# Keys and queries of finished batches made inside the state space chunks, convolution diagonals streamed, pieces laid out anew: one core of Trainium2

## The chip, the cores and the metric

The kernel runs on one core of a Trainium2 chip, in float32 throughout. The metric is the device time of one execution in microseconds (us). The engines are PE (TensorE: matmuls; its weight loads are listed as PEld), DVE (VectorE), ACT (ScalarE), POOL (GpSimd) and SP (SyncE, which issues all DMAs here). Each runs its own list of instructions in order, and they wait for one another by semaphores.

## The reference, cut to what matters

x has 4 batches of 384 channels and 64 x 64 positions (4096 tokens).

```python
def _gn(v, G=32): ...                    # normalize in 32 groups of channels, per batch
# layer 0: state space layer over the 4096 tokens of a batch
xn = layernorm(_gn(x)); xb, z = split(xn @ in_proj_w.T)      # 2 x 768 channels
xc = silu(causal_conv4(xb) + conv_b)                         # 4 taps, per channel
dt, B, C = split(xc @ x_proj_w.T); dt = softplus(dt @ dt_w.T + dt_b)
h = exp(dt * A) * h + (dt * xc) * B                          # 16 states a channel, token by token
x = x + out_proj((sum_n h * C + xc * D) * silu(z))
# layer 1: attention over a 7 x 7 window around each position, 12 heads of 32
q, k, v = split(w_qkv @ _gn(x) + b_qkv); q = q * 32**-0.5    # k, v padded by 3, edges repeated
x = x + w_proj @ softmax(q . k_window + rel_bias) . v_window + b_proj
```

## The kernel before

**State space layer** (`state_space_layer`, line 328). A batch is cut into 11 chunks of 372 or 376 tokens, so there are 44 chunks. A chunk has 24 groups: 6 blocks of 128 channels (d) times 4 groups of 4 states (g). For a group, `drive` (776) multiplies dt * xc with B, on DVE or POOL as the table DRIVES says (quarters are states of a group); `decay` (794) makes exp(dt * A) on ACT, one of three PSUM banks at a time; `scan` (805) runs four recurrences on DVE; `times_c` (820) multiplies with C on POOL; `sums` (834) adds up the states by transposing matmuls on PE. Around it, per chunk: normalization (`gn`, `ln_*`), `in_proj` (569) with weights streamed from DRAM by `load_w` (565), `conv` (602) as four matmuls with diagonal matrices `dcv` that stay in SBUF, `x_proj`, `dt_mm`, `softplus`, `gate`, `out_proj` (689), `residual` (706), which stores the layer's result x1 to DRAM.

The order of the work is written out by hand: every piece has a tick in the table AT (line 40), relative to its chunk's first scan; 16 ticks are one group, 384 one chunk. `put` (447) collects the pieces, they are sorted by tick, and each engine gets its instructions in that order. `Written` (133; line 143 is where every instruction is recorded, hence the L143 in the profile) keeps this order on each engine, SP's DMAs among them. PSUM has three banks `mm` for all matmuls but the scans' (`bank`, 430).

Statistics of the next batch's x (`x_stats`, `x_norm`) and of a finished batch's x1 (`out_norm`) are made within the chunks, in eight steps over PE, DVE, POOL and ACT (`stats_phases`, 247). Values of the attention for batches that are finished are made within the chunks too: three tiles of 128 tokens a chunk, from chunk 13 on (`value_load` 485 to `value_store` 513, the loop over `tiles`), and go to DRAM (`vdr`).

**Attention** (`attention_layer`, 999). There are 32 stripes of 8 rows (512 tokens), each of 12 units: 4 pairs of 8 x 8 blocks times 3 sets of 4 heads. A unit's steps are spread over the loop at 1261: `scores` (1183: lg matmuls on PE, bias and minimum on DVE, exp on ACT), `divide` (1207: POOL) one step later, `turn` (1212: transposes pt on PE, copies pT on DVE and ACT) two steps later, `weigh` (1223: ov on PE) three later. Beside the units, `pieces` (1149) sets matmuls for other stripes: values (where they are not made yet), three `key` (1074) and two `query` (1104) pieces of stripe s+2, the third query of s+1, and three `project` pieces of s-1. A piece is three matmuls of 128 x 512 in the single bank `mm`; one float32 matmul is two records in the profile. `key` is followed by copies on POOL that repeat edges and hand rows to the neighbouring stripes. `load_x` brings x1 of stripe s+3, and POOL normalizes it (`gn`, 1055). `load_v` (1246) brings the values of a pair of blocks in four DMAs.

Of the kernel before, what the change touches and what calls it, by code (L numbers as in the profile page):

```python
# [8 lines left out]
F32 = mybir.dt.float32  # L9
# [5 lines left out]
P = 128  # L15
# [21 lines left out]
HBUFS = 6  # L37


AT = dict(  # L40
    load_x=(-766,),
    gn=(-732, -677, -738),
    ln_mean=(-636,),
    ln_centre=(-633,),
    ln_square=(-611, -560, -597),
    ln_var=(-545, -545, -544),
    ln_rstd=(-520,),
    ln_scale=(-516,),
    halo=(-551,),
    load_w=(-473, -410, -373, -353, -313, -350, -153, -130, -112, -106, -67, -22),  # L50
    in_proj=(-416, -404, -346, -331, -272, -290, -122, -108, -84, -43, -41, -1),
    in_bias=(-402, -388, -344, -328, -268, -283, -122, -104, -65, -40, -36, 49),
    conv=(-374, -299, -281, -232, -218, -226),
    conv_bias=(-358, -296, -280, -230, -162, -217),
    silu_x=(-245, -127),
    x_proj=(-123, -114),
    x_rows=(-112,),
    dt_mm=(-93, -59),
    softplus=(-87, -58),
    load_b=(-77, -46, -18, -33),  # L60
    load_c=(-6, 17, 47, 65),
    silu_z=(4, 79),
    gate=(142, 234, 270, 319, 399, 457),
    out_proj=(500, 518, 565, 589, 571, 605),
    load_res=(430, 476, 582),
    residual=(529, 591, 621),
    out_stats=(678, 680, 704),
    dt_to_bank=(-50, 10, 100, 156, 201, 264),
    dt_times_x=(-43, 31, 110, 163, 208, 297),
    dtx_copy=(-16, 49, 126, 165, 231, 317),  # L70
    skipped=(17, 109, 145, 173, 251, 301),
    turned_out=(111, 179, 233, 293, 363, 410),
    back=(125, 224, 247, 306, 386, 447),
    carry=(
        -4, -32, -1, 12, 34, 59, 38, 72, 102, 116, 126, 142, 171, 188, 188, 221, 239, 238,
        250, 276, 290, 296, 318, 326,
    ),
    last_states=(
        25, 39, 49, 73, 82, 97, 112, 134, 155, 159, 173, 202, 209, 238, 239, 257, 280, 292,
        310, 324, 344, 357, 372, 388,  # L80
    ),
    times_c=(
        31, 40, 65, 89, 107, 114, 131, 135, 182, 191, 197, 205, 226, 242, 251, 265, 298, 302,
        320, 345, 354, 373, 396, 398,
    ),
    sums=(
        47, 70, 91, 97, 120, 134, 143, 175, 183, 217, 222, 227, 247, 262, 282, 283, 312, 318,
        342, 347, 378, 390, 400, 406,
    ),
    x_stats=(-37, 71, 89, 302),  # L90
    x_norm=(24, 252, 265, 310, 322, 334, 336, 342, 352),
    out_norm=(332, 414, 421, 427, 436, 466, 473, 479, 499),
    value_load=(31, 188, 279),
    value_norm=(68, 213, 341),
    value_mm=(84, 236, 362),
    value_out=(125, 243, 385),
    value_store=(217, 245, 400),
# [3 lines left out]
    (-5, 1, "G", 0, 4), (-4, 0, "V", 0, 3), (-4, 0, "V", 3, 1), (7, 2, "V", 0, 4),  # L101
    (14, 3, "G", 0, 4), (52, 4, "G", 3, 1), (54, 4, "V", 0, 2), (63, 4, "V", 2, 1),
    (71, 6, "V", 0, 4), (76, 5, "V", 3, 1), (78, 5, "G", 0, 3), (89, 7, "G", 0, 4),
    (112, 8, "V", 0, 4), (132, 10, "G", 0, 2), (134, 9, "G", 2, 2), (136, 9, "V", 0, 2),
    (136, 10, "V", 2, 1), (147, 11, "G", 0, 4), (152, 10, "G", 3, 1), (173, 12, "V", 0, 4),
    (191, 14, "V", 0, 4), (200, 13, "G", 0, 4), (222, 15, "G", 0, 4), (252, 16, "V", 0, 4),
    (256, 17, "V", 0, 1), (257, 18, "V", 0, 3), (264, 17, "G", 1, 3), (276, 18, "G", 3, 1),
    (292, 19, "G", 0, 4), (298, 20, "V", 0, 4), (323, 22, "V", 0, 3), (325, 22, "V", 3, 1),
    (330, 21, "V", 2, 2), (332, 21, "G", 0, 2), (350, 23, "G", 0, 4),
# [50 lines left out]
def two_layers(  # L160
# [147 lines left out]
    have_values = set()  # L308
# [19 lines left out]
    def state_space_layer(eng):  # L328
# [5 lines left out]
        with ExitStack() as es:  # L334
# [6 lines left out]
            w_dt = wt.tile([P, DI], F32, name="w_dt")  # L341
            dcv = wt.tile([P, ND, KC, P], F32, name="dcv")
# [3 lines left out]
            w_v = wt.tile([P, NJ, C], F32, name="w_v")  # L346
            fill = wt.tile([QB, KN], F32, name="fill")
            ge.memset(fill, MASKED)
            with tc.tile_pool(name="fold", bufs=1, side="right") as fold, tc.tile_pool(
# [16 lines left out]
                for k in range(3):  # L366
                    dq.dma_start(w_dt[32 * k : 32 * k + DTR, :], dt_wT)
# [33 lines left out]
                for m in range(2 * ND):  # L401
                    dq.dma_start(wdr[m], w_in[:, :, m * P : (m + 1) * P])
                for d in range(ND):
                    for k in range(KC):
                        ve.tensor_scalar(
                            dcv[:, d, k, :], ident, w_cv[:, d, k : k + 1], None, ALU.mult
                        )

# [107 lines left out]

            def xn_of(X, j):
                return made[X]["xn"][:, j, HALO : HALO + chunks[X][3]]
# [82 lines left out]

            def conv(X, d):
                T = chunks[X][3]
                made[X]["cv", d] = ps = bank()
                xb = made[X].pop(("xb", d))
                for k in range(KC):
                    te.matmul(
                        ps[:, :T], dcv[:, d, k, :], xb[:, k : k + T],
                        start=(k == 0), stop=(k == KC - 1),
                    )  # L610
                done(xb)

# [45 lines left out]
            def dt_mm(X, half):  # L658
                T = chunks[X][3]
                for k in range(3):  # L660
# [4 lines left out]
                        ps[:, :T], w_dt[rows, d * P : (d + 1) * P], made[X]["xd"][rows, :T],  # L665
# [212 lines left out]
            for X in range(len(chunks)):  # L878
# [18 lines left out]
                for d in range(ND):  # L897
                    piece("conv", d, conv, d)
                    piece("conv_bias", d, conv_bias, d)
# [85 lines left out]

            put(-120, dq.dma_start, w_out, out_wT.rearrange("(k p) m -> p k m", p=P))
            put(-120, dq.dma_start, w_v, qkv_wT[:, 2 * C :].rearrange("(k p) m -> p k m", p=P))
            put(
# [10 lines left out]
    def attention_layer(eng, gm1, qkb, pjb):  # L999
# [3 lines left out]
        with ExitStack() as es:  # L1003
# [5 lines left out]
            dq.dma_start(w_qkv, qkv_wT.rearrange("(k p) m -> p k m", p=P))  # L1009
# [64 lines left out]
            def key(s, m, ps):  # L1074
                b, r = of(s)
# [11 lines left out]
                )  # L1087
                own = kt[:, m, PAD : PAD + RB, :]
# [59 lines left out]

            def pieces(s, k):

                b, r = of(s + 2)
                if (b, NPAIR * r) in have_values:
                    table = {
                        0: [(query, s + 1, 2)], 2: [(key, s + 2, 0)], 4: [(key, s + 2, 1)],
                        5: [(project, s - 1, 0)], 6: [(key, s + 2, 2)],
                        7: [(project, s - 1, 1)], 9: [(project, s - 1, 2)],
                        10: [(query, s + 2, 0)], 11: [(query, s + 2, 1)],
                    }
                else:
                    table = {  # L1160
                        0: [(query, s + 1, 2), (value, s + 2, 0)],
                        1: [(value, s + 2, 1)], 2: [(value, s + 2, 2)], 3: [(value, s + 2, 3)],
                        4: [(key, s + 2, 0)], 5: [(project, s - 1, 0)],
                        6: [(key, s + 2, 1)], 7: [(project, s - 1, 1)],
# [191 lines left out]
```

## Time and profile before

| what | us |
|---|---|
| runs of the kernel | 6871.43, 6875.25, 6876.22 (median 6875.25) |
| the profiled execution's own time | 6870.13 |
| its span, first to last instruction | 6868.4 |
| first scan of the state space layer begins | 124.2 |
| its last scan ends | 5145.3 |
| first scores of the attention begin | 5211.7 |

Busy time over the span: PE 6287.1 us (92%), PEld 4236.8 (62%), DVE 5869.3 (85%), ACT 5609.8 (82%), POOL 5710.1 (83%). By stages (us, and the mean granted clock of TensorE as a share of full speed):

| stretch | length | PE | PEld | DVE | ACT | POOL | clock | DMA share |
|---|---|---|---|---|---|---|---|---|
| 124.2 to 5145.3 | 5021.1 | 4518.0 | 3224.5 | 4923.3 | 4548.5 | 4955.5 | 0.96 | 0.32 |
| 5145.3 to 5211.7 | 66.4 | 53.9 | 30.3 | 8.9 | 5.2 | 20.4 | 0.89 | 0.39 |
| 5211.7 to 6868.4 | 1656.7 | 1629.7 | 926.2 | 906.0 | 1016.7 | 726.7 | 1.00 | 0.31 |

The busy time of an engine is the time in which at least one of its instructions runs. Instructions of one engine overlap by about 0.1 us, and matmuls are pipelined and their ends modelled, so a sum of durations is more than the time they take together. Registers, branches, semaphores and DMA issues are not counted as busy. `h<-h,BC` reads: tile h is written from tiles h and BC. The chain that ended last goes through DVE's scans (h, 24% of the span), PE's matmuls into mm (24%) and POOL's h (9%); since it follows each wait to the one who ended it, it wanders between engines that are all nearly full.

### The profile page before, as it was taken

Reading aid. Unit: us, or ns where it says so; the run is one execution under the profiler, and the core shown is the slowest. Engines: PE = TensorE matmul, PEld = TensorE weight load, DVE = VectorE, ACT = ScalarE, POOL = GpSimd, SP = SyncE. Lnnn points to the kernel's source line nnn. Section 1 sums busy time; section 2 is a strip of 40 time slices with the busy share of each in tenths; the row PEclk is TensorE's granted clock in tenths of the full one; section 3 lists DMA queues with packets and bytes.
Section 4 is the critical chain, followed back from the end, with each engine's and each line's share of the span. In section 5 each row is a group of like instructions: output and inputs, shape, how many; then the busy total and the mean of one; then the engine's idle time right before and its main releaser. Section 6 shows DMA issues by size and latency. Waiting matters only on the chain.

```text
span 6868.4 us, 132032 instructions
## 1 busy us (share of the span) xinstructions
PE 6287.1 (92%) x46986; PEld 4236.8 (62%) x46986; DVE 5869.3 (85%) x10215; ACT 5609.8 (82%) x13919; POOL 5710.1 (83%) x2701
## 2 busy tenths in 40 slices
PE   7898988898999999899999999999969999999999
PEld 4666666666666666666666666666655555555555
DVE  4999999999999999999999999999994555555555
ACT  4898988889999989899999999999974666665556
POOL 2999999999999999999999999999993444444443
PEclk9999999999999999999999999999989999999999
DMA  5233232223333323333333333333313232333332
GB/s 156 83 104 98 96 102 85 96 92 109 104 112 103 107 97 111 103 107 110 109 104 101 102 95 106 97 107 104 95 60 107 95 100 94 97 99 102 105 101 91
DMA packets 502833, 694.86 MB, mean 101 GB/s; under 512 B 51269, under 2 KB 457173, under 8 KB 502045
## 3 DMA queue, kind: packets, MB, share of 16 engines
q1 hardware_dynamic: 502172, 686.41, 31.6%
q8 instruction: 372, 6.09, 0.4%
q14 instruction: 289, 2.36, 0.1%
HBM read 600.76 MB, written 85.65 MB: 100 GB/s over the span
## 4 chain that ended last, share of the span: by engine, by line
PE 39%; DVE 27%; ACT 17%; POOL 9%; issue 6%; DMA 1%; SPq 0%; POOLq 0%; DVEq 0%; ACTq 0%
DVE h L143 24%; PE mm L143 24%; POOL h L143 9%; PE yps L143 5%; ACT da L143 5%; PE pt L143 5%; ACT L143 4%; PE lg L143 3%; PE ov L143 2%; ACT sg L143 1%; ACT dt L143 1%; ACT sz L143 1%; ACT xc L143 1%; DVE dtxps L143 1%; DVE yg L143 1%
## 5 line engine op out<-in xcount | busy, mean ns | idle before, releaser
L143 DVE TENSOR_TENSOR_SCAN h<-da,h 128x373 f32<-128x373 f32 (+1 forms) x4224 | 3650.2, 913 | 90.1 <-ACT da L143 68.9
L143 POOL TENSOR_TENSOR h<-h,BC 128x1488 f32<-128x1488 f32 (+1 forms) x1056 | 3252.1, 3105 | 40.9 <-ACT state L143 24.9
L143 ACT ACTIVATE da<-dt,nega 128x372 f32<-128x372 f32 (+1 forms) x4224 | 2369.2, 570 | 260.4 <-DVE h L143 229.0
L143 POOL TENSOR_TENSOR h<-dtx,BC 128x1488 f32<-128x1488 f32 (+3 forms) x704 | 1770.5, 2526 | 40.5 <-ACT dtx L143 38.7
L143 PE MATMUL yps<-ident,h 128*124 128x128 f32 (+1 forms) x12672 | 1600.3, 279 | 215.9 <-POOL h L143 214.9
L143 PEld LDWEIGHTS yps<-ident,h 128*124 128x124 f32 (+1 forms) x12672 | 1468.1, 143 | 422.2 <-POOL h L143 278.7
L143 PE MATMUL mm<-xn,w_in 128*128 128x372 f32 (+3 forms) x3168 | 1201.1, 519 | 186.2 <-ACT dt L143 165.3
L143 POOL TENSOR_TENSOR sg<-sg,rs 128x784 f32<-128x784 f32 x384 | 573.3, 1493 | 682.4 <-DVE rs L143 554.9
L143 ACT ACTIVATE sg<-sg,mx 128x196 f32<-128x196 f32 x1536 | 685.2, 447 | 463.5 <-DVE mx L143 458.9
L143 PEld LDWEIGHTS mm<-xn,w_in 128*128 128x128 f32 x3168 | 615.0, 205 | 581.2 <-ACT dt L143 215.9
L143 DVE TENSOR_TENSOR h<-dtxps,BC 128x1488 f32<-128x1488 f32 (+6 forms) x836 | 937.6, 1134 | 11.0 <-ACT dtx L143 5.0
L143 DVE CUSTOM_DVE_ANT_0 sg<-lg,bias 128x196 f32<-128x196 f32 x1536 | 464.3, 358 | 277.2 <-PE lg L143 276.9
L143 PE MATMUL mm<-xb,dcv 128*128 128x372 f32 (+1 forms) x2112 | 690.5, 476 | 0.0
L143 ACT ACT_TABLE_LOAD x529 | 678.7, 1283 | 9.6 <-PEq L1341 0.8
L143 PE MATMUL mm<-yg,w_out 128*128 128x372 f32 (+1 forms) x1584 | 531.8, 477 | 0.0
L143 PEld LDWEIGHTS mm<-xb,dcv 128*128 128x128 f32 x2112 | 389.0, 190 | 227.2 <-DVE yg L143 3.3
L143 PE MATMUL mm<-xp,w_qkv 128*128 128x512 f32 x1098 | 501.7, 593 | 0.0
L143 PE MATMUL pt<-ident,sg 128*98 128x128 f32 x3072 | 429.6, 279 | 16.7 <-ACT pT L143 11.3
L143 PEld LDWEIGHTS pt<-ident,sg 128*98 128x98 f32 x3072 | 315.3, 128 | 150.8 <-issue 102.9
L143 PEld LDWEIGHTS mm<-yg,w_out 128*128 128x128 f32 x1584 | 291.3, 191 | 162.4 <-issue 0.6
L143 PEld LDWEIGHTS ov<-pT,vw 98*32 98x32 f32 x12288 | 189.2, 110 | 237.3 <-issue 162.5
L143 POOL COPY kt<-kt 128x210 f32<-128x210 f32 (+1 forms) x384 | 97.3, 286 | 250.7 <-ACT kt L143 244.8
(134 smaller groups left out, 6896.3 us busy)
## 6 DMA issues: line engine op xcount, KB each, us to landing
BC<-bcrows SPq DMA_DIRECT2D x320, 744.0 KB
w_in<-wdr SPq DMA_DIRECT2D x528, 192.0 KB
vw<-vdr SPq DMA_DIRECT2D x512, 147.0 KB
xs<-in_x_dram SPq DMA_DIRECT2D x210, 186.0 KB
xp<-x SPq DMA_DIRECT2D x32, 768.0 KB
o<-x SPq DMA_DIRECT2D x96, 256.0 KB
out_dram<-o SPq DMA_DIRECT2D x96, 256.0 KB
BC<-bcrows SPq DMA_DIRECT2D x32, 752.0 KB
```

What stands on the lines that cost most here:

```text
L143: ins = made(*args, **kw)
```

## The change

There are five parts. One: for batches 0 to 2, as far as chunks are there, a tile of 256 tokens of keys and one of queries is made in each chunk from two chunks after the batch's end on: x1 is loaded, normalized on ACT, multiplied with weights that are loaded 128 columns at a time, evacuated on ACT and stored to DRAM (`kdr`, `qdr`; queries in the order in which blocks read them, with bias and scale). Two: in the attention, a stripe whose keys and queries are there loads them (`load_keys`) at unit 0 two stripes ahead, and has no x1 load, no normalization and no key and query pieces; POOL's edge copies become `surround`. Three: the diagonals `dcv` are stored to DRAM once and loaded per chunk and block (`load_cv`, three buffers); the weights of dt are kept in a third of the room. Four: the loads of `w_qkv` and `w_pj` and the output bias come later. Five: all ticks in AT, and DRIVES, are new.

```diff
 AT = dict(
-    load_w=(-473, -410, -373, -353, -313, -350, -153, -130, -112, -106, -67, -22),
-    in_proj=(-416, -404, -346, -331, -272, -290, -122, -108, -84, -43, -41, -1),
+    load_w=(-556, -419, -340, -366, -306, -365, -138, -149, -106, -103, -67, -32),
+    in_proj=(-411, -388, -340, -343, -251, -321, -128, -134, -80, -33, -46, 23),
...
-    x_norm=(24, 252, 265, 310, 322, 334, 336, 342, 352),
-    out_norm=(332, 414, 421, 427, 436, 466, 473, 479, 499),
+    x_norm=(12, 182, 194, 198, 211, 231, 247, 257, 271),
+    out_norm=(319, 401, 414, 424, 442, 465, 482, 493, 507),
...
+    load_cv=(-473, -346, -314, -235, -259, -344),
+    key_load=(44, 213),
+    key_norm=(93, 69, 126, 276, 234, 288),
+    key_mm=(135, 139, 181, 303, 305, 348),
+    key_out=(143, 150, 191, 307, 315, 358),
+    key_store=(289, 467),
 DRIVES = (
...
+                dcv = fold.tile([P, ND, KC, P], F32, name="dcv")
                 for d in range(ND):
                     for k in range(KC):
                         ve.tensor_scalar(
                             dcv[:, d, k, :], ident, w_cv[:, d, k : k + 1], None, ALU.mult
                         )
+                    dq.dma_start(ddr[d], dcv[:, d, :, :])
...
+            def key_load(cell):
+                b, k = cell["at"]
+                xk = cell["x"] = tile_of([P, NJ, KT], "xk", 1)
+                dq.dma_start(
+                    xk, x1s[b][:, k * KT : (k + 1) * KT].rearrange("(k p) t -> p k t", p=P)
+                )
+            def key_norm(cell, j):
+                g = gm1[cell["at"][0]]
+                v = cell["x"][:, j, :]
+                se.activation(v, v, AF.Identity, scale=g[:, j, 1:2], bias=g[:, j, 2:3])
+            def key_weights(cell, m):
+                w = cell["w", m] = tile_of([P, NJ, P], "wk", 2)
+                at = cell["part"] * C + m * P
+                dq.dma_start(w, qkv_wT[:, at : at + P].rearrange("(k p) m -> p k m", p=P))
+            def key_mm(cell, m):
+                if m != 1:
+                    cell["ps", m // 2] = bank()
+                lo, w = KT if m == 1 else 0, cell.pop(("w", m))
+                for j in range(NJ):
+                    te.matmul(
+                        cell["ps", m // 2][:, lo : lo + KT], w[:, j, :],
+                        cell["x"][:, j, :], start=(j == 0), stop=(j == NJ - 1),
+                    )
...
+            def key_out(cell, m):
...
+                if cell["part"]:
+                    se.activation(
+                        cell["y"][:, m, :], ps[:, lo : lo + KT], AF.Identity,
+                        bias=qkb[:, NJ + m : NJ + m + 1],
+                    )
+                else:
+                    se.activation(
+                        cell["y"][:, m, :].rearrange("p (b r c) -> p r b c", b=NBLK, c=CB),
+                        ps[:, lo : lo + KT].rearrange("p (r b c) -> p r b c", b=NBLK, c=CB),
+                        AF.Identity, bias=qs[:, m : m + 1], scale=HD**-0.5,
+                    )
...
+            def load_cv(X, d):
+                made[X]["cw", d] = w = tile_of([P, KC, P], "cw", CWBUFS)
+                dq.dma_start(w, ddr[d])
...
+            for i, (part, have) in enumerate(((1, have_keys), (0, have_queries))):
+                tiles = [(b, k) for b in range(NB - 1) for k in range(L // KT)]
+                for X in range(len(chunks)):
+                    if not tiles or X < NCHUNK * (tiles[0][0] + 1) + 2:
+                        continue
+                    b, k = tiles[0]
+                    if k % 2 == 0 and X == len(chunks) - 1:
+                        break
+                    cell = {"at": tiles.pop(0), "part": part}
+                    have.add((b, k))
...
+            def load_keys(s):
+                b, r = of(s)
+                dq.dma_start(
+                    q_of(s),
+                    qdr[b][:, r * TX : (r + 1) * TX].rearrange("(k p) t -> p k t", p=P),
+                )
+                for m in range(NJ):
+                    dq.dma_start(
+                        kt_of(s)[:, m, PAD : PAD + RB, PAD : PAD + HW],
+                        kdr[b][m * P : (m + 1) * P, r * TX : (r + 1) * TX].rearrange(
+                            "p (r c) -> p r c", r=RB
+                        ),
+                    )
...
+                if 0 <= stripe + 2 < stripes and has_keys(stripe + 2):
+                    if k == 0:
+                        load_keys(stripe + 2)
+                    if k in (4, 6, 8):
+                        surround(stripe + 2, (k - 4) // 2)
-                if k == 2 and 0 <= stripe + 3 < stripes:
+                if k == 2 and 0 <= stripe + 3 < stripes and not has_keys(stripe + 3):
                     load_x(stripe + 3)
```

The whole of the convolution's, the keys' and the attention's functions stand above as they were before. In DRIVES, the quarters on DVE go from 49 in 19 instructions to 50 in 21, those on POOL from 47 in 16 to 46 in 19. `key_store` stores a tile of keys in one DMA and one of queries in three; `key_weights` is due 32 ticks ahead of its matmuls. `conv` takes its diagonals from the tile `cw` that `load_cv` filled.

## The prediction

> **What bounds the kernel now.** I read three views in this order: the table of busy time by stretches, the groups of the instructions, and TensorE's instructions in order of time. The first, for three neighbouring chunks of the state space layer, and for single stripes of the attention (columns: stretch, length, then busy us and count of PE, PEld, DVE, ACT, POOL, then granted clock, DMA share, GB/s):
>
> ```profile
> 4472.60:4585.30 112.70, 104.13 (x537) 74.38 (x536) 111.30 (x137) 105.25 (x239) 112.59 (x41) 0.97 0.33 103
> 4585.30:4697.90 112.60, 104.00 (x536) 74.26 (x535) 111.23 (x136) 105.17 (x239) 112.53 (x41) 0.97 0.33 103
> ...
> 803.40:915.80 112.40, 97.81 (x501) 69.33 (x500) 111.98 (x140) 101.48 (x227) 112.34 (x41) 0.97 0.30 98
> ...
> 6792.34:6829.08 36.74, 35.07 (x697) 21.41 (x690) 25.41 (x124) 29.45 (x112) 17.92 (x12) 1.00 0.36 112
> 5453.85:5503.81 49.96, 49.37 (x732) 27.94 (x726) 27.72 (x127) 31.85 (x115) 23.10 (x27) 1.00 0.31 98
> ```
>
> A chunk is POOL: 112.59 of 112.70 us busy, DVE 1.3 us behind, and it repeats to 0.1 us. ACT has 7.4 us idle in it, PE 8.6. The chunk at 803 makes no values yet; the one at 4472 makes three tiles of them, which cost PE 6.3 and ACT 3.8 us, and the chunk grew by 0.3. The whole layer, from its first scan at 124.2 to its last at 5145.3, takes 5021 us; 44 such chunks would take 4959, so 62 us are stalls, most where a batch's statistics are made.
>
> The attention (5211.7 to 6868.4) is PE: 49.37 of 49.96 us in a stripe that makes its keys and queries. The first row of its two is a stretch near the end, where nothing but the output projection is left to make: 36.74 us. TensorE there, in order of time:
>
> ```profile
> 6813.96 0.60 PE L143 MATMUL lg<-kt,q 32*64 32x196 f32 x16
> 6814.49 0.64 PE L143 MATMUL pt<-ident,sg 128*98 128x128 f32 x4
> 6815.42 0.64 PE L143 MATMUL pt<-ident,sg 128*98 128x128 f32 x4 [0.29 <-ACT pT L143]
> 6815.99 0.65 PE L143 MATMUL ov<-pT,vw 98*32 98x64 f32 x32
> 6816.57 0.60 PE L143 MATMUL lg<-kt,q 32*64 32x196 f32 x16
> ...
> 6825.83 2.74 PE L143 MATMUL mm<-aT,w_pj 128*128 128x512 f32 x6
> 6828.50 0.65 PE L143 MATMUL ov<-pT,vw 98*32 98x64 f32 x32
> 6829.08 0.60 PE L143 MATMUL lg<-kt,q 32*64 32x196 f32 x16
> ```
>
> A unit with no piece of projection beside it takes 2.5 us (start of lg to start of lg; 2.61 here), with PE waiting now and then for ACT's copy pT. A piece of three matmuls (six records, 2.74 us) makes a pair of units longer by about 2.2.
>
> **The change, part by part.** From the code: key tiles are made in chunks 13 to 42, one of keys and one of queries in each (16 of batch 0, 14 of batch 1; the last chunk starts no pair). That covers stripes 0 to 14.
>
> *1. Attention, stripes 0 to 13.* Pieces of stripe s make keys and queries of s+2, so stripes 0 to 12 lose all six pieces, stripe 13 one. Units' starts give 42.31 us for stripe 0 and 49.95 to 50.09 for 1 to 12. After: 12 x (49.96 - 36.74) = 158.6 saved. Stripe 0 has no projection and becomes 12 x 2.5 = 30, and 2 for the output bias's small matmuls put there (2.06 now): 10 saved. Stripe 13 loses 4.7 - 2.5 = 2.2. Sum -171. PE loses 6 x 2.57 = 15.4 us in such a stripe, and I take 13.2, since the wait for pT comes up as the pieces go; the row above already holds it. New there is that POOL's copies of key edges now wait for a DMA, not for ACT. The load is issued at a stripe's unit 0, POOL wants it at unit 4, 10 us later. Ahead of it SP has four loads of values (0.72 us of SP each), three of the residual (0.41) and the queries' (0.38): 4.5 us, so it lands 8 to 10 us after unit 0. If it is late, POOL's divide queues behind the copy, and PE's transposes behind that. Between 0 and 2 us a stripe, 0 to 26; I take 0, because a divide needs only 1.49 us of a 2.5 us unit.
>
> The load's rows are 256 bytes, 3072 packets a stripe. Packets of 512 bytes took 27 ns and of 1536 bytes 65 ns of one of 16 engines, so less than 3072 x 27/16 = 5.2 us a stripe, at a DMA share of 0.36: hidden.
>
> *2. Start of the attention.* Now the last x store is issued at 5166.8, and the first scores begin at 5211.71, after ten pieces of keys and queries (5179 to 5212). After, they need the statistics (PE and POOL done at 5175.5), bias, two stripes of keys, queries, and 24 edge copies on POOL (1.08 us for four, 6.5). Some 4.3 MB must land; this stretch had 120 to 137 GB/s at a DMA share of 0.38 to 0.39, so 310 to 360 GB/s at a full one: 12 to 14 us from 5168, and with issue, landing and the last copies about 5190. -22, between -15 and -28.
>
> *3. Start of the kernel.* SP runs its list in order. It issues the first chunk's xn at 38.73 now, and ACT normalizes it at 50.22. After, six stores of the convolution's diagonals stand ahead, each waiting for DVE's dcv, which runs from 49.85 to 54.64. So xn is issued near 55.5 and there at 60 to 62. DVE's centring (55.74) comes 9 to 11 us later: +10, between +4 and +16.
>
> *4. A chunk with keys.* PE gets 18 matmuls of 256 columns, 36 records. Six of 512 take 2.74 us, 0.17 of it the last one's tail: 0.43 each, so 0.215 at 256 and 7.7 us a chunk. ACT gets six normalizations of 128x256 (xv's 128x128 take 481 ns, xn's 128x372 take 690, so 590, less 0.1 of overlap with the next: 0.49) and six evacuations (564 at 372 from PSUM, so 0.46, less 0.1): 5.1 us. SP gets 18 DMAs, 0.3 to 0.7 us each, 5 to 13 us; its own waits hold 1313 us for DVE's residual alone between 1800 and 4800. DMA gets 4.3 MB beside 11.6, a share of 0.33 going to about 0.45.
>
> So PE's 8.6 and ACT's 7.4 us of idle time must cover 7.7 and 5.1. From below: nothing is late, 0. From above: nothing is hidden, 7.7 a chunk, 231 in 30 chunks. The nearest row is the values: 6.3 on PE and 3.8 on ACT cost 0.3. I take 1.0 a chunk, three times that, as less room is left: +30.
>
> The Trainium skill's page "Perfetto Trace Analysis", section "Identifying the Most-Contended Engine", holds that matmul busy time says little about TensorE's headroom and that weight-load busy time is to be used. By its rule 74.4 of 112.7 us, 66%, leaves room for all of it, the term is 0 and the sum further down is -186; by the matmul row, only 0.9 of 8.6 us would be left, and the term and the -156 stand.
>
> *5. Drives.* The new list gives VectorE 50 quarters in 21 instructions (49 in 19 before) and POOL 46 in 19 (47 in 16). By the groups (V: 1684, 1297, 907, 523 ns for four to one quarters; G: 3362, 2570, 1781, 992), less 0.08 of overlap each, DVE gets 0.5 us a chunk and POOL loses 0.3 to 0.4. POOL's floor falls to 112.3; DVE, 112.0 in chunks that also take a later batch's statistics, rises to 112.5 there. I take +7 over 44 chunks, between -15 and +22.
>
> *6. Statistics.* Steps of x_norm and out_norm are now 9 to 20 ticks apart (one tick is 0.29 us) where some were 2 to 7. Of the 62 us of stalls I take 10 away, between 0 and 50.
>
> **Sum.** -171 - 22 + 10 + 30 + 7 - 10 = -156. The profiled execution has 6870.13 us (span 6868.4), so 6714; the median shown is 5.1 above it, so 6719.
>
> **Rivals.**
> - *ACT's or PE's order sets the chunk.* DVE's scans take decay factors that ACT makes at most three ahead, and ACT's list is in order: a normalization queued ahead of one delays the scan. For it: ACT would be 110.4 of 112.7 busy, and the ACT work that the new ticks put into a chunk's first quarter, by the same rows, is 105% of its time (98% before). Against: DVE waited for ACT only 2.3 us in three chunks. Half the added PE and ACT time showing is 3.2 us a chunk, 96 and not 30: 6785; 4.8 a chunk gives 6833.
> - *PE becomes the bound, and it is slower.* Place: the sums behind each key matmul in PE's list; if they are late, h buffers come free late and POOL's drives wait. Price 7.7 a chunk, 231 and not 30: 6920. It decides from (186 / 30 =) 6.2 us a chunk on.
> - *Nothing shows, and the stalls go too.* Part 4 costs 0, part 6 gives 50, part 5 gives -15: 6627.
> - *It saves less than it says in the attention:* key loads late by 2 us a stripe, 6745; inside the forecast.
>
> **How the numbers follow.** Forecast (6680 to 6760) 0.62; ACT's or PE's order (6760 to 6861) 0.22; better (6600 to 6680) 0.08; slower 0.06; no change 0.02. The range leaves out the slower case, no change, and the outer ends of the two next to it: 6650 to 6830. A measurement tells 0.2% (14 us) from no change: faster 0.92, same 0.02, slower 0.06.
>
> **What would show it.** Stripes 1 to 12 at 36 to 38 us (over 40: the key loads are late, and POOL's wait for kt will be long). First scores at 5211 plus the layer's change, less 22. First scan near 134. Chunks 15 to 18 at 113 to 114.5; at 117 and above with idle DVE before scans the first rival holds, with PE never idle the second. I am wrong if the layer grows by over 100 us.

## The result, and the profile after

| | runs, us | median | ratio to before (95%) |
|---|---|---|---|
| before | 6866.81 to 6876.22 | 6873.34 | |
| after | 6765.22, 6764.37, 6749.24, 6756.08 | 6760.23 | 0.9835 [0.9818, 0.9852] |

The kernel became 113 us faster; it stands 41 us above the 6719 that was forecast. The profiled execution, the slowest of the four, took 6765.22 us (span 6763.5), 104.9 below the profiled one of before and 51 above the 6714 of the forecast's sum. The 104.9 is the number to take apart, because it can be cut into stages. Stretches of the changed kernel (columns: stretch, length, busy us and count of PE, PEld, DVE, ACT and POOL, granted clock, DMA share, GB/s):

```profile
137.70:5227.30 5089.60, 4731.08 (x24217) 3410.38 (x24216) 4955.87 (x6149) 4682.28 (x10527) 4949.96 (x1933) 0.97 0.41 129
5227.30:5270.10 42.80, 19.70 (x94) 13.59 (x91) 5.75 (x14) 0.99 (x4) 9.66 (x22) 0.76 0.52 121
5270.10:6763.50 1493.40, 1450.59 (x22950) 847.45 (x22950) 875.02 (x4028) 985.91 (x3635) 701.01 (x804) 0.99 0.39 118
```

The ends of these stretches are the first scan, the last scan, the first scores and the last instruction. Against the table of before: the first scan comes 13.5 us later, the layer is 68.5 longer, the gap to the first scores 23.6 shorter, the attention 163.3 shorter. 13.5 + 68.5 - 23.6 - 163.3 = -104.9. Three of the four stand within 8 us of what was forecast (+10, -22, -171); the layer was given +27. So the question is where 68.5 us of the layer come from.

A chunk with keys, four neighbouring ones (25 to 28) as a stretch of each kernel, before and after:

```profile
2982.44:3437.91 455.47, 416.76 (x2130) 297.00 (x2129) 450.10 (x558) 421.55 (x952) 450.74 (x162) 0.97 0.35 108
```

```profile
3031.48:3494.14 462.66, 445.48 (x2279) 321.62 (x2278) 454.55 (x565) 439.03 (x998) 449.15 (x173) 0.99 0.47 144
```

PE got 28.7 us in four chunks (7.2 a chunk; 7.7 was forecast), ACT 17.5 (4.4; 5.1 forecast), and the stretch grew by 7.2. All four engines are now over 94% busy and none is at 100%: in such a stretch no single engine's busy time gives the length, and it must be found which order of work leaves the gaps.

In the twelve stripes that lost their pieces, the attention does what the late stripes did before. Here is stripe 3 as a stretch, and the starts of two neighbouring units on PE, both of the changed kernel:

```profile
5377.55:5414.29 36.74, 35.06 (x697) 21.40 (x691) 25.46 (x124) 29.45 (x113) 20.80 (x25) 1.00 0.52 154
```

```profile
5348.13 0.60 PE L152 MATMUL lg<-kt,q 32*64 32x196 f32 x16
...
5350.57 0.60 PE L152 MATMUL lg<-kt,q 32*64 32x196 f32 x16
```

This unit is 2.44 us and the stripe 36.74, to the hundredth the length of the late stripe in the prediction. Stripes 1 to 12 took 36.74 to 39.97, 37.2 on average.

### The profile page after: what moved, and what is told of

It reads as the page before. It is cut to its first block, busy times and chain, and to the rows that moved or that the text cites. A ratio compares the mean times of both kernels' runs of the same rounds, so it can differ in the third digit from the quotient of the medians.

```text
span 6763.5 us, 135265 instructions
## 1 busy us (share of the span) xinstructions
PE 6286.7 (93%) x47526; PEld 4326.7 (64%) x47526; DVE 5867.9 (87%) x10258; ACT 5708.1 (84%) x14235; POOL 5668.5 (84%) x2788
## 4 chain that ended last, share of the span: by engine, by line
PE 43%; ACT 21%; DVE 20%; issue 6%; POOL 6%; DMA 3%; SPq 1%; POOLq 0%; DVEq 0%; ACTq 0%
PE mm L152 28%; DVE h L152 17%; PE yps L152 7%; ACT da L152 6%; POOL h L152 6%; PE pt L152 4%; ACT L152 4%; ACT sg L152 3%; PE ov L152 2%; PE lg L152 2%; DMA w_in<-wdr 2%; ACT dt L152 1%; ACT sz L152 1%; ACT xb L152 1%; ACT pT L152 1%
## 5 line engine op out<-in xcount | busy, mean ns | idle before, releaser
L152 POOL TENSOR_TENSOR h<-dtx,BC 128x372 f32<-128x372 f32 (+5 forms) x836 | 1757.9, 2113 | 51.7 <-ACT dtx L152 41.2
L152 PEld LDWEIGHTS yps<-ident,h 128*124 128x124 f32 (+1 forms) x12672 | 1453.5, 142 | 261.2 <-POOL h L152 165.8
L152 PE MATMUL mm<-xn,w_in 128*128 128x372 f32 (+3 forms) x3168 | 1146.5, 503 | 102.4 <-DMA w_in<-wdr 47.7
L152 DVE TENSOR_TENSOR h<-dtxps,BC 128x1488 f32<-128x1488 f32 (+5 forms) x924 | 964.5, 1059 | 6.5 <-ACT dtx L152 4.6
L152 PE MATMUL mm<-xb,cw 128*128 128x372 f32 (+1 forms) x2112 | 697.8, 476 | 7.1 <-DMA cw<-ddr 5.1
L152 PEld LDWEIGHTS mm<-xb,cw 128*128 128x128 f32 x2112 | 389.8, 189 | 239.2 <-DVE h L152 6.0
L152 PE MATMUL pt<-ident,sg 128*98 128x128 f32 x3072 | 447.6, 281 | 29.5 <-ACT pT L152 21.3
L152 PE MATMUL mm<-xk,wk 128*128 128x256 f32 x1080 | 268.3, 390 | 46.2 <-ACT dt L152 46.2
L152 ACT ACTIVATION_READ_ACCUMULATOR sg<-sg,mx 128x1 f32 x1536 | 288.2, 188 | 0.0
```

What stands on the lines that cost most here:

```text
L152: ins = made(*args, **kw)
```

## The experiments

Each run is listed with the length of its stages ("gap" is from the last scan to the first scores) and the mean length of chunks 2 to 7 (no values, no keys), 0 to 12 (no keys) and 13 to 42 (keys), from its one trace. "Time" is the median of four or five runs for before, after, e2, e4, e8 and e10; the others ran once.

| kernel | time | first scan | layer | gap | attention | 2-7 | 0-12 | 13-42 |
|---|---|---|---|---|---|---|---|---|
| before | 6873.34 | 124.2 | 5021.1 | 66.4 | 1656.7 | 112.82 | 113.58 | 114.47 |
| after | 6760.23 | 137.7 | 5089.6 | 42.8 | 1493.4 | 114.54 | 115.11 | 116.07 |
| e1 | 6893.96 | 134.1 | 5032.4 | 68.0 | 1657.6 | 114.84 | 114.84 | 114.29 |
| e2 | 6712.31 | 135.7 | 5045.3 | 41.9 | 1493.0 | 113.34 | 113.81 | 115.16 |
| e3 | 6907.32 | 135.0 | 5045.2 | 68.8 | 1656.3 | 113.26 | 113.84 | 115.18 |
| e4 | 6745.66 | 122.7 | 5091.4 | 42.1 | 1490.2 | 114.68 | 115.00 | 116.18 |
| e5 | 6864.57 | 134.3 | 5000.0 | 69.2 | 1659.4 | 112.71 | 113.51 | 113.77 |
| e6 | 6698.52 | 132.7 | 5029.4 | 42.3 | 1492.3 | 112.71 | 113.40 | 114.79 |
| e7 | 6707.63 | 133.4 | 5038.9 | 40.9 | 1492.8 | 112.70 | 113.40 | 115.12 |
| e8 | 6698.73 | 120.1 | 5046.0 | 41.9 | 1493.4 | 113.34 | 113.61 | 115.27 |
| e9 | 6848.46 | 122.2 | 4995.6 | 69.6 | 1659.3 | 112.68 | 113.42 | 113.66 |
| e10 | 6696.94 | 124.5 | 5034.4 | 42.2 | 1493.0 | 112.68 | 113.55 | 114.91 |
| e11 | 6694.12 | 134.7 | 5023.2 | 41.7 | 1492.9 | 113.34 | 113.73 | 114.44 |
| e12 | 6672.05 | 134.3 | 5002.0 | 41.4 | 1492.7 | 112.70 | 113.76 | 113.73 |

How finely this can be read: chunks 2 to 7 come out at 112.7 in some kernels and at 113.34 in three (e2, e8, e11) that run the same code there. Kernels that run the same chunks throughout (after and e4, e2 and e8) differ by 0.1 in the last column and by 1.8 and 0.7 us in the layer. I take differences under 0.6 a chunk in the column 2-7, under 0.3 in the column 13-42 and under 8 us in the layer of one trace as not readable. The first scan scatters by 5 us among kernels that start alike.

**What I saw before the first four runs.** Chunks 2 to 7 make no keys and yet grew by 1.7 us. PE, SP, ACT and DVE of the changed kernel, in order of time, in chunk 4 (start, duration, then what the idle time before it waited for):

```profile
606.21 2.06 PE L152 MATMUL mm<-xn,w_in 128*128 128x375 f32 x6
611.53 3.63 PE L152 MATMUL mm<-xn,w_in 128*128 128x375 f32 x6 [3.27 <-DMA w_in<-wdr]
```

```profile
605.09 0.39 SPq L152 DMA_DIRECT2D xn<-in_x_dram  x1
605.53 0.95 SPq L152 DMA_DIRECT2D cw<-ddr  x2
606.53 0.43 SPq L152 DMA_DIRECT2D w_in<-wdr  x1
```

```profile
615.19 0.57 ACT L152 ACTIVATE xb<-mm,binp 128x375 f32<-128x375 f32 x1 [1.84 <-PE mm L152]
```

```profile
616.26 1.76 DVE L152 TENSOR_TENSOR_SCAN h<-da,h 128x373 f32<-128x373 f32 x2 [1.25 <-ACT da L152]
```

The load of the third block of in_proj's weights is due at tick -340, and so are its matmuls; before, the load had 27 ticks ahead. In SP's list it stands behind the next xn and two of the new loads of diagonals, is issued at 606.53, and PE begins on it 5.0 us later. PE is late, so ACT's evacuation of that block is late, the decay factors queue behind it on ACT, and DVE's next scan waits. None of that was in the prediction.

**e1, the changed kernel without key and query tiles** (the attention makes its own, as before):

```diff
-                tiles = [(b, k) for b in range(NB - 1) for k in range(L // KT)]
+                tiles = []
-                if s == 2 * UNITS:
+                if s == 2 - 3 * UNITS:
```

> No keys or queries are made in the chunks; ticks, drives and streamed diagonals of the changed kernel stay, and the attention makes all keys and queries itself as before. The layer grew by 68.5 us, 20 of it in chunks 0 to 12, which make no keys. Theory 1 (the new layout costs about 1.5 us in every chunk, the key work next to nothing): chunks 14 to 18 and 25 to 28 stay between 114.3 and 115.3 us (115.6 with keys), the layer at 5070 to 5090, the whole near 6930 to 6945. Theory 2 (the key work costs 1.5 us or more, by PE or ACT, the first chunks have another cause): those chunks fall to 113.9 or less, the layer to 5040 or less, the whole near 6895. Theory 3 (the diagonals' DMAs delay other loads) expects of this run what theory 1 does.

The layer took 5032.4, so keys cost 57 us here, 1.8 a chunk, as the second theory said. Chunks 2 to 7 stayed at 114.84: what makes them long is not the keys. In the attention the 163 us are gone, as they should be.

**e2, the late load mended** (its tick earlier by 21, some 6 us):

```diff
-    load_w=(-556, -419, -340, -366, -306, -365, -138, -149, -106, -103, -67, -32),
+    load_w=(-556, -419, -361, -366, -306, -365, -138, -149, -106, -103, -67, -32),
```

> The changed kernel with one tick changed: the load of the third weight block of in_proj is due at -361, not -340, which is the tick of the matmul that uses it; SP thus issues it ahead of the next chunk's x and two diagonals. Theory 1a (a part of the layout's cost is this load, on which PE waits 3.3 us in each chunk without keys): PE's wait for w_in falls under 1 us a chunk, chunks 2 to 7 go from 114.5 to 113.0 to 113.7, key chunks by 0 to 0.5, the whole by 15 to 35 us. Theory 1b (the layout costs by other places, PE had the time): the wait goes, the chunks stay within 0.3 us. Theory 3 (DMA traffic): the wait moves to other blocks and the chunks stay.

6712.31 us [ratio to before 0.9753 to 0.9783], 48 us below the changed kernel, more than the 15 to 35 expected. One number in a table was worth 0.7% of the time. 17 us of it lie in chunks 0 to 12 and 27 in 13 to 42. Over the whole layer, from the first scan to the last, three waits follow it: DVE's for decay factors, POOL's for state copies (both made by ACT) and PE's for w_in. From the waits of the changed kernel and of e2 (us in total, times, longest):

```profile
POOL h L152 <- ACT state L152: 110.7, 149, 2.7
DVE h L152 <- ACT da L152: 109.7, 202, 4.2
...
PE mm L152 <- DMA w_in<-wdr: 47.3, 24, 3.7
```

```profile
DVE h L152 <- ACT da L152: 73.0, 161, 1.8
...
POOL h L152 <- ACT state L152: 68.3, 99, 2.8
...
PE mm L152 <- DMA w_in<-wdr: 3.4, 1, 3.4
```

PE's 44 us of waiting for w_in are gone, and with them 37 us of DVE's and 42 of POOL's. I read this as one stall seen at three places, since the layer is 44 us shorter. Part by part the sums do not match: PE's wait for w_in lost 26 us in chunks 0 to 12 and 18 in chunks 13 to 42. The price is shown by the runs, and once more by e4 and e8 below, which differ in the same tick: 45.4 us of layer.

**e3, the kernel before with streamed diagonals and nothing else changed:**

```diff
+    load_cv=(-420, -360, -330, -296, -274, -278),
-            dcv = wt.tile([P, ND, KC, P], F32, name="dcv")
+                dcv = fold.tile([P, ND, KC, P], F32, name="dcv")
+                    dq.dma_start(ddr[d], dcv[:, d, :, :])
-                        ps[:, :T], dcv[:, d, k, :], xb[:, k : k + T],
+                        ps[:, :T], cw[:, k, :], xb[:, k : k + T],
```

> The kernel before, with its ticks and drives, without keys in the chunks; only the diagonals are streamed, as in the changed kernel, 26 to 60 ticks ahead of their use. Theory 1 (layout): chunks stay at 112.7 to 113.1 us where nothing else disturbs, the layer at 5015 to 5035, and only the start is later by 10 to 14, so 6880 to 6900 in all. Theory 3 (the stream's 1.6 MB a chunk delay other loads): chunks of 114 us and more, the layer at 5070 or above, 6935 or more in all.

The layer grew by 24 us, between the two expectations. POOL's waits for the B and C rows in chunks 14 to 18, of the kernel before and of e3, fit this reading: the old ticks leave SP's list no room for six more loads a chunk where I put them. They grew by 7.3 us, and these five chunks by 7.5.

```profile
POOL h L143 <- DMA BC<-bcrows: 1.8, 1, 1.8
```

```profile
POOL h L144 <- DMA BC<-bcrows: 9.1, 4, 3.4
```

So 24 is the price of the stream at these ticks, not of the stream; e9 asks again with the new ones.

**e4, the six stores of the diagonals issued by POOL instead of SP:**

```diff
-                    dq.dma_start(ddr[d], dcv[:, d, :, :])
+                    ge.dma_start(ddr[d], dcv[:, d, :, :])
```

> The changed kernel with the six stores of the diagonals issued by POOL's queue instead of SP's. The theory of the start (SP stands behind DVE's diagonals with the first chunk's x behind it): x is issued near 40, ACT normalizes it near 51 and DVE centres it near 56 and not 66.7, the first scan begins at 126 to 130 and not 137.7, the whole is 8 to 12 us less. Rival (the order of the first chunk's pieces makes the start late): the first scan gains under 4 us.

First scan at 122.7 instead of 137.7, 6745.66 by the median (14.6 less), more than expected. Some of that is scatter: the eight kernels of the table that start like the changed one (after, e1, e2, e5, e6, e7, e11, e12) have their first scan at 132.7 to 137.7, the three with the stores on POOL (e4, e8, e10) at 120.1 to 124.5, and the means are 12.2 apart. SP, ACT and DVE at the start, changed kernel:

```profile
50.55 4.24 SPq L152 DMA_DIRECT2D ddr<-dcv  x6
...
56.12 0.49 SPq L152 DMA_DIRECT2D xn<-in_x_dram  x1
```

```profile
61.17 1.87 ACT L152 ACTIVATE xn<-xn,gm 128x372 f32<-128x372 f32 x3 [13.23 <-DMA xn<-in_x_dram]
```

and e4:

```profile
39.43 0.48 SPq L152 DMA_DIRECT2D xn<-in_x_dram  x1
```

```profile
49.62 1.88 ACT L152 ACTIVATE xn<-xn,gm 128x372 f32<-128x372 f32 x3 [2.08 <-POOL gm L152]
```

With SP's list free, xn is issued 10 us before ACT takes it, and what ACT waits for last is the statistics (gm); with the stores ahead of it in the list, ACT sits idle for 13.23 us and waits for xn.

**e5, both: load mended, no keys** (the edits of e1 and e2 together).

> The changed kernel with the load of in_proj's third weight block due earlier (as e2_w2_early) and without keys and queries in the chunks; the attention makes them. With the late load still there, taking the keys away saved 1.7 us a chunk. If the two costs are independent, chunks 14 to 18 and 25 to 28 fall from 114.9 to 113.2 and chunks 2 to 7 stay at 113.3; if the keys cost only because PE was already late from that load, they fall by 0.7 or less, to 114.2 or above. The layer at 4990 to 5000 against 5015 to 5030.

The layer takes 5000.0, 21 less than before the change. So the new layout by itself is a gain, though it carries the stream; keys cost 45 us (5045.3 - 5000.0), 1.4 in each of 30 chunks; the late load costs 44 (5089.6 - 5045.3). The two are not independent: with the late load still there the keys cost 57 (e1), and without keys the late load costs 32 (5032.4 - 5000.0), so 12 us belong to both. Chunks 14 to 18 and 25 to 28 fell from 114.86 to 113.67, between the two expectations. The waits that e2 was read by fall once more without the keys; the same two of e5:

```profile
DVE h L152 <- ACT da L152: 46.0, 130, 1.8
...
POOL h L152 <- ACT state L152: 30.4, 50, 1.1
```

Where does the layout's gain lie? In both kernels the steps of the statistics fall into chunks 8, 12, 13, 19, 23, 24, 30, 34 and 35. These nine chunks together lost 15.5 of the 21 us from before to e5; chunk 20, which has no such step, lost 4.3; the plain chunks 36 to 41 stayed (113.11 and 113.16 on average). Chunk 23 as a stretch, before and in e5:

```profile
2747.92:2866.09 118.17, 105.20 (x543) 74.46 (x542) 113.08 (x142) 104.97 (x235) 112.20 (x40) 0.97 0.34 105
```

```profile
2748.45:2862.03 113.58, 104.99 (x545) 74.75 (x544) 112.99 (x145) 105.48 (x237) 110.81 (x46) 0.98 0.38 124
```

DVE's busy time is the same and 4.5 us of waiting are gone. What it waited for in the kernel before was not a step of the statistics. SP, PE and DVE there:

```profile
2819.21 9.34 SPq L143 DMA_DIRECT2D vdr<-vo  x15
2828.65 0.35 SPq L143 DMA_DIRECT2D w_in<-wdr  x1
```

```profile
2831.06 3.56 PE L143 MATMUL mm<-xn,w_in 128*128 128x372 f32 x6 [3.08 <-DMA w_in<-wdr]
```

```profile
2835.72 1.76 DVE L143 TENSOR_TENSOR_SCAN h<-da,h 128x373 f32<-128x373 f32 x2 [3.15 <-ACT da L143]
```

A block of in_proj's weights stands behind 15 stores of values in SP's list, PE waits 3.08 us for it, and DVE's scan is late. Chunk 34 shows the same, with 3.3 us. From chunk 1 to chunk 43 these two chunks are the only ones in which PE waits for w_in in the kernel before, and e5 has none. They lost 4.6 and 3.5 us, 8.1 of the 15.5. So at least there the gain is again that of a load's place in a list; what gained the rest is not shown.

**e6, e7, e11 and e12 take the keys apart**, all on top of e2. e6 leaves out ACT's normalization, e7 two of three matmuls, e11 both, and e12 all of it but the DMAs:

```diff
-                se.activation(v, v, AF.Identity, scale=g[:, j, 1:2], bias=g[:, j, 2:3])
+                pass
```

```diff
-                for j in range(NJ):
+                for j in range(1):
```

and for e12, where a tile is loaded and stored as it is:

```diff
-                    te.matmul(
-                        cell["ps", m // 2][:, lo : lo + KT], w[:, j, :],
...
+                done(cell.pop(("w", m)))
...
-                yk = cell.pop("y")
+                yk = cell.pop("x")
```

> As e2_w2_early, but the six normalizations of key tiles on ACT are left out of every chunk (keys and queries are then made from x1 without its group normalization): ACT has 3 us a chunk less to do, PE and the DMAs the same. Theory ACT (the keys cost because ACT's list delays decay factors): chunks 14 to 18 and 25 to 28 fall from 114.9 by 0.8 to 1.5. Theory PE (the keys cost because PE's list is full): by less than 0.3. Theory DMA (loads are late): by less than 0.3.

> As e2_w2_early, but of each key or query matmul over 384 channels only the first 128 are multiplied (two thirds of the key matmuls are left out): PE has 5.1 us a chunk less to do, ACT and the DMAs the same. Theory PE: chunks 14 to 18 and 25 to 28 fall from 114.9 by 0.8 to 1.5, the state copies before POOL's work come earlier. Theory ACT: by less than 0.3. Theory DMA: by less than 0.3.

> As e2_w2_early, with both things left out at once: the six key normalizations (ACT 3 us a chunk) and two thirds of each key matmul (PE 5.1 us a chunk); a third of the matmuls, the six evacuations and all DMAs remain. Chunks 13 to 42 took 115.2 us with everything, 114.8 without the normalizations, 115.1 without the matmuls, 113.7 with the DMAs alone. If each engine's load is paid by itself, the two savings add: 114.6 to 114.8. If PE and ACT hold each other up (an evacuation waits for its matmul, a matmul for its normalization, with decay factors and sums queued behind), more goes than the sum: 114.3 or less. If the evacuations' places are the price, 114.7 or above.

> As e2_w2_early, but of the key work in the chunks only the DMAs remain: x1 and the weights are loaded and x1 itself is stored in place of keys and queries (no normalization, matmuls or evacuations of keys in the chunks; x1 tiles have two buffers). Theory DMA (transfers and SP's queue make the keys' price): chunks 14 to 18 and 25 to 28 stay at 114.5 or above, as with everything (114.9). Theory ACT and PE together (neither alone gave more than 0.7 us): they fall to what they are without keys, 113.5 to 113.9.

Chunks 25 to 28 as one stretch, in e5 (no keys), e12 (their DMAs alone), e2 (all), e6, e7 and e11:

```profile
2977.78:3433.06 455.28, 417.92 (x2137) 293.90 (x2136) 451.79 (x565) 423.77 (x953) 449.60 (x173) 0.99 0.38 123
```

```profile
2983.03:3437.31 454.28, 416.25 (x2137) 293.34 (x2136) 451.75 (x565) 423.19 (x953) 449.56 (x173) 0.99 0.48 147
```

```profile
2999.73:3459.14 459.41, 442.06 (x2282) 318.85 (x2281) 452.91 (x565) 439.61 (x1000) 449.85 (x173) 1.00 0.48 146
```

```profile
2987.54:3446.54 459.00, 443.67 (x2282) 320.58 (x2281) 453.61 (x566) 430.51 (x978) 449.89 (x173) 0.99 0.48 146
```

```profile
2992.23:3450.37 458.14, 429.10 (x2186) 303.81 (x2185) 453.05 (x566) 439.53 (x1001) 449.96 (x173) 0.99 0.48 146
```

```profile
2991.18:3446.43 455.25, 426.36 (x2184) 300.95 (x2183) 452.17 (x566) 429.81 (x976) 449.37 (x173) 0.99 0.48 146
```

The DMAs cost nothing that can be read: e12 moves 147 GB/s where e5 moves 123, and is no longer (113.73 against 113.77 in chunks 13 to 42). Without the normalizations ACT is 9 us less busy and the stretch 0.4 shorter; without two matmuls in three PE is 13 us less busy and it is 1.3 shorter. Over all 30 key chunks these are 0.37 and 0.04 a chunk; the first is just above the 0.3 that can be read, the second can't be read. Both together give 0.72, more than the sum by about as much as can be read; e11's 114.44 falls between its two expectations (114.3 or less, and 114.6 to 114.8). In the chunks that the expectations name (14 to 18 and 25 to 28), e2 has 114.86, e6 114.63, e7 114.60, e11 113.99 and e12 113.85. So neither theory of one engine held, with its 0.8 to 1.5, and DMA is out. Neither engine alone sets the price; what is left (113.73 to 114.44, another 0.7) belongs to the evacuations, the matmuls that stayed and the waits between them.

**e8, the mended load and the stores on POOL together** (the edits of e2 and e4).

> Both mends together, everything computed: the load of in_proj's third weight block due at -361 (alone: 6712 us) and the diagonals' stores issued by POOL's queue (alone: first scan 15 us earlier, the whole 15 us less). They touch different stages, so they should add: 6694 to 6702, first scan at 120 to 124, chunks as in e2_w2_early. If part of the late load's price was paid in the first chunk, 6704 to 6710.

6698.73 us, ratio 0.9746 [0.9733, 0.9759]: the two add up (-48 and -14.6 from 6760.23 would be 6697.6). Here the order that the keys enter can be seen. ACT and DVE of e8 around the end of chunk 36's softplus:

```profile
4339.80 1.28 ACT L152 ACT_TABLE_LOAD   x1
4341.10 0.58 ACT L152 ACTIVATE da<-dt,nega 128x372 f32<-128x372 f32 x1
...
4344.08 0.57 ACT L152 ACTIVATE sz<-mm,binp 128x372 f32<-128x372 f32 x1
4345.37 0.48 ACT L152 ACTIVATE yk<-mm,qs 128x256 f32<-128x256 f32 x1 [0.72 <-PE mm L152]
4345.75 0.19 ACT L152 COPY state<-h 128x4 f32<-128x4 f32 x1
4345.84 0.57 ACT L152 ACTIVATE da<-dt,nega 128x372 f32<-128x372 f32 x1
```

```profile
4341.78 1.76 DVE L152 TENSOR_TENSOR_SCAN h<-da,h 128x373 f32<-128x373 f32 x2 [0.64 <-ACT da L152]
...
4346.44 2.58 DVE L152 TENSOR_TENSOR_SCAN h<-da,h 128x373 f32<-128x373 f32 x3 [0.81 <-ACT da L152]
```

ACT has just spent 2.6 us on two table loads around softplus, and is behind. At 4344.65 it comes to the evacuation yk, waits 0.72 us for PE to end the query matmuls, and only then makes the state copy and the decay factor that stand behind yk in its list; DVE's scan waits 0.81 for that factor. Here PE and ACT are late together, which fits that taking work from one of them alone helps so little. It is one place in one chunk; that the keys' 1.4 us a chunk come about like this is argued, not shown.

**e9, e5 with the diagonals kept in SBUF as before.** There is no such kernel with keys: it lacks 5.5 KB a partition, and so the diagonals are streamed.

```diff
-                dcv = fold.tile([P, ND, KC, P], F32, name="dcv")
-                    dq.dma_start(ddr[d], dcv[:, d, :, :])
+            dcv = wt.tile([P, ND, KC, P], F32, name="dcv")
```

> As e5_w2_keys_off, but the convolution's diagonals stay in SBUF and are not streamed (with keys there is no room for them). It tells what the stream costs under the new layout: with the old ticks it cost 24 us over the layer, 1.5 a chunk where values are made, half a us elsewhere. If the new layout has found room for it, the layer is within 8 us of e5_w2_keys_off and the start 10 to 13 us earlier; if not, chunks 14 to 18 are 1 us or more shorter and the layer 20 us or more.

The layer took 4995.6, so under the new ticks the stream costs 4.4 us, inside the scatter, and 12.1 at the start (134.3 - 122.2), as much as e4's edit gives back.

**e10, key steps moved off the scans that wait**, on e8: three normalizations to other ticks, one evacuation 5 later.

```diff
-    key_norm=(93, 69, 126, 276, 234, 288),
-    key_out=(143, 150, 191, 307, 315, 358),
+    key_norm=(100, 108, 126, 262, 234, 270),
+    key_out=(143, 150, 191, 307, 320, 358),
```

> As e8_w2_diag_pool, with the same work placed elsewhere in ACT's list: two key normalizations due after the silu of z and not just ahead of it, two ahead of the softplus by 18 to 32 ticks and not by 6 to 18, one evacuation 5 ticks later, since ACT was seen to wait 0.7 us for its matmul with state copies and decay factors queued behind. Theory ACT's order (what the keys cost in a chunk is decay factors and state copies that come late behind table loads and waiting evacuations): DVE's waits at the 20th, 75th and 79th scan of a chunk go, 0.3 to 1.0 us a chunk, 10 to 30 us of the whole against e8_w2_diag_pool. Theory of shared room (the chunk is limited by the sum of all engines' work): within 5 us of it.

Waits in chunks 36 to 41, of e8 and of e10:

```profile
DVE h L152 <- ACT da L152: 15.7, 39, 0.8
...
POOL h L152 <- ACT state L152: 14.3, 21, 1.3
```

```profile
DVE h L152 <- ACT da L152: 12.4, 43, 0.8
...
POOL h L152 <- ACT state L152: 11.6, 16, 1.1
```

The waits fell by 6 us in six chunks, but the median by 1.8 only, which these runs can't tell from nothing. That is the 5 us at most of the theory of shared room, not the 10 to 30 of ACT's order. It may be that work moved from one crowded place on ACT makes another one crowded; no run shows it. At 6696.94 (0.9745 [0.9732, 0.9758]) it is as fast as e8, and both are faster than either kernel of this case: 63 us below the changed one.

## Why the prediction was right, and where a step failed

1. *Attention, -171:* -163.3, by the means forecast. Of the 7.7 missing, 5.6 lie in a few stripes above 36.74 (stripe 4 took 38.19, stripe 8 39.97) and 1.8 in stripe 0, which took 33.77 and not 32. In stripes 4 and 8 PE stands still once for 1.5 us with nothing in the profile that it waits for; why is open. The possible wait for late key loads, 0 to 26 with 0 taken, was right: in POOL's waits between 5350 and 5700 there is `kt`, and it is small.

```profile
POOL kt L152 <- DMA kt<-kdr: 4.7, 6, 1.9
```

2. *Start of the attention, -22:* -23.6. PE's last wait before the first scores, 14.59 us, is for a load of keys, as the prediction had it.
3. *Start of the kernel, +10:* +13.5, by the mechanism given (xn issued at 56.12, forecast 55.5), and e4 takes it away by that mechanism alone. Over the eight kernels that start like this it is +10.4 on average.
4. *Keys in a chunk, +30 (1.0 each):* +45 (1.4 to 1.5), inside its bounds of 0 to 7.7. Its nearest row, the values at 0.3, had been tripled for "less room"; it should have been multiplied by five. The mechanism looks like a small form of the first rival, not at its 3.2 to 4.8: with the keys DVE waits 27 us longer for ACT's decay factors (73.0 in e2, 46.0 in e5) and POOL 38 longer for its state copies. What makes ACT late is not shown: its normalizations alone are 0.37 a chunk (e6), and a better order for them gained nothing that can be read (e10). The second rival, PE as the bound, is out: in e7 PE lost 13 us of busy time in four chunks and they became 1.3 shorter, and over all key chunks it gained 0.04 a chunk. That also bears on the Trainium skill's rule ("Perfetto Trace Analysis", section "Identifying the Most-Contended Engine"). Matmul busy time was 445.48 of 462.66 us in key chunks, 96%, and still was not the limit, which agrees with the page; weight-load busy time was 321.62, 70%. But what the rule gave as a sum, 0 for the keys, was off by 45: room on PE in total did not say what the added work costs where ACT waits for a matmul, as for the 0.72 us in e8.
5. and 6. *Drives +7, statistics -10, together -3:* -21 (before to e5), the stream of diagonals included, for which the layer had been charged nothing; without it -25.5 (e9). That is better than I took, and inside the range of part 6, 0 to 50. But the prediction put most of the 62 us of stalls where statistics are made; the nine chunks with their steps are together 30 us longer than nine of 112.7, about half. And of what was gained, 8.1 us belong to weights late in SP's list (chunks 23 and 34), so that spacing out the steps, the reason given in part 6, is not shown to have gained the rest.

**What failed** is that the sum of the layer had no term for the streams' order: part 4 counted SP's 18 new DMAs and part 3 the stores at the start, but no part compared, load by load, the tick of each new `load_w` with the tick of its matmul, though the diff shows both lists and the third entry of each is -340. That term was +44, nearly as much as the keys'. So the layer is -21 + 45 + 44 = +68 (or, taken in the other order, -21 + 57 + 32) where -3 + 30 = +27 was forecast; the keys cost 15 more than forecast and the layout saved 18 more, which nearly cancels, so that the miss is about the size of the missing term. The sign that I gave, chunks 15 to 18 at 113 to 114.5, shows it: they took 115.4 to 116.0. The result, 6760.23, lies 0.2 us above the forecast's 6680 to 6760, at the very foot of the first rival's span, and inside the range of 6650 to 6830. That it stayed in the range is in part luck: a cost that stood in none of the cases was no larger, and two other misses had opposite signs.

What stays open: how the keys' price comes about, of which half goes with the normalizations and two thirds of the matmuls and half does not; and how much of the new layout's -25.5 is DRIVES, how much the statistics' steps and how much the place of the loads, which were not run apart.

## What to carry to other kernels

When all ticks are new, go through every load and hold its tick against that of its first user, and count what stands ahead of it in the issuing queue; a lead of 0 instead of 27 ticks cost 44 to 48 us in a kernel whose engines are 94 to 98% busy, as much as all the work added to the layer. The kernel before already had two such late loads (chunks 23 and 34). Where four engines were nearly full, idle time in total did not price added work here, and taking half of it from one engine gave back little; look at what stands behind it in each list, and test it, since moving the steps by hand gained nothing here (e10). Stores that come in front of a first load can be moved to another engine's queue; here they cost 12 us on SP's and nothing that can be read on POOL's.

## What the runs showed of the hardware that was not expected

DMAs of many short rows, issued one behind another, hold SP's queue for long; I had priced all of SP's new DMAs at 0.3 to 0.7 us. SP's DMAs of key tiles and of query tiles in the changed kernel (duration in ns: least, median, most; first and last start):

```profile
L152 SPq DMA_DIRECT2D kt<-kdr x45: 432/2225/4956, 5252.0 to 5722.1; - x45
```

```profile
L152 SPq DMA_DIRECT2D qdr<-yk x90: 360/3040/4448, 1768.0 to 5123.4; - x90
```

Both kinds are issued three in a row: loads of 1024 rows of 256 bytes, stores of 1024 rows of 128 bytes. The first of three took 0.36 to 0.84 us of SP, hardly more than the 0.43 (median) of the load of queries, 384 rows of 2 KB, just ahead of the key loads. The second and third took 2.0 and 3.9 us on average for the loads, 3.3 and 3.4 for the stores. So the length comes with what stands ahead, and not with the rows of the DMA alone; why is not shown. The stores were hidden here: e12 has them and its layer is as long as that of e5, which has none. For the loads no run tells.

The granted clock in chunks 25 to 28 was 0.97 before and 0.99 in e1 and in e5, which have no keys either, so it is not the added matmuls that raise it. It does not follow PE's longest wait for one thing in those chunks either: that was 3.0 us before, and 1.6 in the changed kernel, 2.2 in e1 and 3.2 in e5, all three at 0.99. The Trainium skill's page "TensorE: Matmul & The Clock Gate", section "HAM oscillation — how this bites in real kernels", wants no idle gaps of PE above about 3.4 us; all of these waits lie below that, and no run here shows what raised the clock.
